# Who issues the reads of turned attention weights, who loads and mixes a filter's branches, and in what order TensorE takes its work

## The chip, the cores and the metric

The kernel runs on one core of one Trainium2 chip. The time is device microseconds of one execution. Each core has TensorE (PE; its weight loads are listed as PEld), VectorE (DVE), ScalarE (ACT), GpSimd (POOL) and SyncE (SP), each with an instruction queue of its own that is worked off in order. A DMA is issued by an instruction in such a queue: here mostly SP's, some ScalarE's, a few GpSimd's. "Landing" is when all its bytes have arrived.

## What is computed

An image x of 2 x 128 x 64 x 64 goes through a group norm and a first layer (7 x 7 neighbourhood attention with layer norms and three small linear maps; it isn't touched by the change). The result, seen as 2 sequences of 4096 tokens with 128 features, goes through a second layer:

```python
t = _to_tokens(x)
t = t + _L1_attn_ref(_ln_t(t))        # whole attention, q = k = v, the diagonal masked
t = t + _L1_ffn_ref(_ln_t(t), ...)    # a spectral filter
```

The attention has no weights: `softmax(q q^T / sqrt(128)) q` over all 4096 tokens, the diagonal set to -1e9. As the scores are symmetric, the weights of block (a, c) of queries and keys, turned (transposed), are those of block (c, a).

The filter convolves the normed tokens with 16 filters (phi) and multiplies each result by a matrix of 128 x 128, once for the sequence and once for the sequence with alternating signs:

```python
out = jnp.einsum('btkd,k,kde->bte', U_plus, s, Mpp)
out = out + jnp.einsum('btkd,k,kde->bte', U_minus, s, Mpm)
```

There are four such branches (four sets of M_u, M_phi_plus, M_phi_minus), each on a shorter part of the sequence, and the outputs are summed with weights from a softmax over four numbers. The kernel mixes the branches' matrices with these weights before the filter is applied.

## The kernel before, in words

The kernel is one program, written with a scheduler: each engine's instructions are put in order by it, by the order in which they were written (an earlier one has the higher priority) and by when it believes their inputs to be there. Two things overrule it. `tc.keep_in_program_order(...)` puts one instruction behind the instruction written just before it on the same engine. `tc.manual_schedule(engines={...})` keeps the written order on the engines named, for all that is written inside it; the first layer (L861) and the convolution at the end (L1658) are written so.

The stages in the trace: the first layer of both images up to about 350 us; the attention of image 0 up to about 780; that of image 1 up to about 1280; a short tail; from about 1330 the filter's convolution, in written order on TensorE, up to the end.

**The attention** (`attention(b, fill)`, L902) goes over the 36 pairs (a, c), a <= c, of eight chunks of 512 tokens, row by row, each pair in four steps j. In a step:

- `coming_of` (L1010) calls `weights` (L917) for the *next* pair: a score matmul into a PSUM bank (`bank`, five buffers; L927, or L936 for a diagonal pair) and an exponential on ScalarE into a quarter of the tile `e` (L932 or L943). In 27 of the 28 pairs off the diagonal (the "far" ones) the last of four quarters is followed by `sent` (L953): the whole megabyte of `e` is written to a DRAM tile `eb`, by a DMA on ScalarE's queue (L956).
- The current pair's product with its weights as they are: "other" (L1049), summed over four steps in one PSUM buffer, then added to `xa` by VectorE (L1066, or copied, L1068). A diagonal pair goes onto "own" instead, the row's sum (L983, in `onto`).
- `pass_on(2)` (L1017) does what is due of earlier pairs. With `at` the step at which a pair's weights were sent: at `at + MOVE` it calls `moved` (L959), four DMAs on SP's queue that read `eb` back into `et` (two buffers) in another layout (L963, pinned); at `at + TURN` `turned` (L968), two transposes of 32 x 32 blocks on VectorE (L972, pinned); from `at + DELAY` on, up to two products a step of the turned weights onto "own" (L983, pinned). The row's last product is followed by `complete` (L986), which adds "own" to `xa` on VectorE (L989).
- `fill()` (L1362) takes one step of other work from generators: first the urgent ones (`after(b, c)`, L1080, for each completed chunk: transposes L1088, statistics with a `pow` on GpSimd L174, apply L191, transposes back L202, ScalarE's copy L1113, the filter's forward transform L1142 and L1155, ScalarE's copies `uo` L1120, GpSimd's sums and differences `ub` L1123, and SP's stores into DRAM `us`, L1127 and L1132), then a list `steps`. A generator that yields None ends the filler's step; one that yields True lets the next in the list go too.

For image 0 the list `steps` holds `drain()` (the rest of the first layer; it makes the buffers `tt[1]`, `tok[1]`, `cm[1]` at its end, L1395 to L1398), `branch_weights()`, `filters()` (the filters' own transform: `pn` loads L1289, matmuls L1325, GpSimd's fb and fn, stores) and `tokens(1)`. For image 1 it holds what was left, and `for_ffn()` (L1438): once chunk 0 of image 1 is through, `filter_matrices` (L1268), then the load of `inv` and the first four sets of blocks `ct` (L1424).

**Mixing** (`mixed`, L1251): for each of four groups of four filters, for plus and minus, for each of four branches i: a DMA on SP's queue loads four matrices, 256 KB, into a tile `st` (two buffers, tag "st"; L1256); GpSimd multiplies it by the branch's weight (L1259 for i = 0, straight into the result; L1263) and adds it to the result (L1264). Two branches make one step of the filler. After plus and minus of a group GpSimd forms their difference and sum (L1276, L1277) and multiplies each filter's matrix by its sigma (L1280, L1281): one more step. That makes 20 steps.

Of the kernel before, what the change touches and what calls it, by code (L numbers as in the profile page):

```python
# [8 lines left out]
F32 = mybir.dt.float32  # L9
AF = mybir.ActivationFunctionType  # L10
ALU = mybir.AluOpType
# [3 lines left out]
P = 128  # L15
# [6 lines left out]
KF = 16  # L22
NBR = 4
MASKED = -1.0e30
MOVE, TURN, DELAY = 3, 7, 8

DIAG = -1.0e6
QSCALE = DH ** -0.5
# [74 lines left out]
def kernel(  # L103
# [16 lines left out]
    nc = tc.nc  # L120
# [756 lines left out]
    with ap_:  # L877
# [24 lines left out]
        def attention(b, fill):  # L902
# [56 lines left out]
            def moved(eb):  # L959

                et = ep.tile([P, 4, 512], F32, tag="et", name="et", bufs=2)
                for q in range(4):
                    tc.keep_in_program_order(nc.sync.dma_start(  # L963
                        out=et[32 * q : 32 * q + 32], in_=eb[:, q].rearrange("(h p) r -> p h r", h=4)
                    ))
                return et
# [12 lines left out]
                nc.vector.tensor_copy(et[:, m], pt)  # L979

            def onto(own, n, out_, e, first, last):
                tc.keep_in_program_order(
                    nc.tensor.matmul(out_, lhsT=tok[b][:, n, :], rhs=e, start=first, stop=last, skip_group_check=True)  # L983
                )

            def complete(a, own):  # L986
                xs = xa[b][:, chunk(a)]
                if a:
                    nc.vector.tensor_tensor(xs, own, xs, ALU.add)  # L989
                else:  # L990
                    nc.vector.tensor_copy(xs, own)
                fill(CHUNKS[a])
# [11 lines left out]
                if (c, t) == (7, 3):  # L1004
                    complete(a, own)

            coming_, late, turns, owns = [], [], [], {}
            step = 0

            def coming_of(a, c, k, left, halves):  # L1010
# [6 lines left out]
            def pass_on(n):  # L1017

                while coming_ and coming_[0][0] + MOVE <= step:
                    at, eb, a, c = coming_.pop(0)  # L1020
                    et = moved(eb)
                    turns.append((at + TURN, et))
                    late.extend((at + DELAY, a, c, et, t) for t in range(4))
                while turns and turns[0][0] <= step:
                    turned(turns.pop(0)[1])
                while n and late and late[0][0] <= step:
                    _, a, c, et, t = late.pop(0)
                    pair_onto(owns[a], a, c, et, t)
                    n -= 1

            es, halves = [], []
            for k in range(4):
                es.append(weights(0, 0, k, es, halves))
            for i, (a, c) in enumerate(pairs):
                following = pairs[i + 1] if i + 1 < len(pairs) else None
                coming, halves = [], []
                if a != c:
                    other = ps_o.tile([P, 512], F32, tag="other", name="other")
                else:
                    owns[a] = ps_o.tile([P, 512], F32, tag="own", name="own", bufs=2)  # L1040
                for j in range(4):
                    if following:
                        coming.append(coming_of(*following, j, coming, halves))
                    n = 4 * CHUNKS[a] + j
                    turn = lambda v, o: v.rearrange(o, q=4) if far(a, c) else v
                    if a == c:
                        onto(owns[a], n, owns[a], es[j], j == 0, a == 7 and j == 3)
                    else:
                        nc.tensor.matmul(  # L1049
                            turn(other, "p (q r) -> p q r"), lhsT=tok[b][:, n, :], rhs=es[j],  # L1050
                            start=(j == 0), stop=(j == 3),
                        )
                    if a != c and not far(a, c):
                        if j == 0:
                            here = ep.tile([P, 4, 512], F32, tag="et", name="et", bufs=2)
                        turned_here(here, es, j)
                        late.append((step + 1, a, c, here, j))
                    pass_on(2)
                    fill()
                    step += 1  # L1060
                if a != c:
                    xs, ov = xa[b][:, chunk(c)], other
                    if far(a, c):
                        xs, ov = xs.rearrange("p (t q j) -> p q t j", t=4, q=4), ov.rearrange("p (q t j) -> p q t j", q=4, t=4)
                    if a:
                        nc.vector.tensor_tensor(xs, ov, xs, ALU.add)  # L1066
                    else:
                        nc.vector.tensor_copy(xs, ov)  # L1068
                es = coming
            while late or coming_:  # L1070
                step += 1
                pass_on(2)
                fill()
            complete(7, owns[7])


        spare = [tok[0][:, 0:4, :]]
# [128 lines left out]
        def branch_weights():  # L1206
# [37 lines left out]
            nc.vector.tensor_tensor(wt, wt, ys, ALU.add)  # L1244

            yield
            for _ in mixed(mu, m_u, nc.vector, False):
                pass
            yield

        def mixed(dst, src, eng, steps):  # L1251
            dst2 = dst.rearrange("p k e -> p (k e)")
            for i in range(NBR):
                st = sp.tile([P, 4, P], F32, tag="st", name="st")
                n = src.shape[1]
                nc.sync.dma_start(out=st[:, 0:n], in_=src[i].rearrange("k d e -> d k e"))  # L1256
                st2 = st[:, 0:n].rearrange("p k e -> p (k e)")
                if i == 0:
                    eng.tensor_scalar(dst2, st2, wt[:, 0:1], None, ALU.mult)  # L1259
                elif eng is nc.vector:  # L1260
                    eng.scalar_tensor_tensor(dst2, st2, wt[:, i : i + 1], dst2, ALU.mult, ALU.add)
                else:
                    eng.tensor_scalar(st2, st2, wt[:, i : i + 1], None, ALU.mult)  # L1263
                    eng.tensor_tensor(dst2, dst2, st2, ALU.add)  # L1264
                if i % 2 and steps:
                    yield
# [218 lines left out]
    with ExitStack() as cv:  # L1485
# [210 lines left out]
        b = NB - 1  # L1696
# [117 lines left out]
```

## Time and profile before

| | |
|---|---|
| median of 3 runs | 2092.68 us (2091.77 to 2095.08) |
| the profiled execution, its own time | 2097.21 us |
| its span, first to last instruction | 2095.5 us |
| mean granted TensorE clock | 0.963 |
| busy: PE, PEld, DVE, ACT, POOL | 1931.1, 1357.0, 910.3, 723.4, 682.4 us |
| chain that ended last, PE's share; POOL; DMA | 63%; 9%; 7% |
| et read issues (L963), SP, count | 216, median 0.42 us each |
| eb write issues (L956), ScalarE, count | 54, median 0.33 us each |
| branch loads (L1256), SP, count | 32 of 256 KB, and 4 of 192 KB |
| turned transposes (L972), VectorE | 108, mean 1.22 us |
| the mixing's multiply (L1263) and add (L1264) on GpSimd | 1.56 and 1.26 us each |

How to read it: an engine's busy time is the union of its instructions; matmuls overlap each other by their fill, so a record of 0.6 us can follow the one before by 0.43. A 32-bit matmul is two records. Idle time before an instruction is put down to what released it last. The granted clock tells what share of TensorE's full speed the throttle let through. A name such as `et<-eb` is output from input.

### The profile page before, as it was taken

The page shows a single profiled execution, that of the slowest core. Times are in us where ns is not written, and L with a number is a line of the kernel's source. Part 1 is how long each engine was busy: PE and PEld are TensorE (multiplying, and loading weights), DVE is VectorE, ACT ScalarE, POOL GpSimd, SP SyncE. Part 2 cuts the span into 40 slices and gives each one's busy share as a digit, 9 for nine tenths or more (in the row PEclk, how much of TensorE's full clock was granted, in tenths as well). Part 3 has the DMA queues.
Part 4 walks back from the last instruction along what each step waited for, and adds up shares of the span by engine and source line. Part 5 has one row for each costly group of instructions (what it writes and reads, how often), then busy time and mean ns, then how long its engine had stood idle before and what let it go on. Part 6 is the DMA issues. An engine that isn't in the chain of part 4 may idle for free.

```text
span 2095.5 us, 51013 instructions
## 1 busy us (share of the span) xinstructions
PE 1931.1 (92%) x20504; PEld 1357.0 (65%) x20504; DVE 910.3 (43%) x2874; ACT 723.4 (35%) x1686; POOL 682.4 (33%) x1054
## 2 busy tenths in 40 slices
PE   6899998998899999995388998999999999999998
PEld 4677775444444444442133444699999899999987
DVE  5799986543433343422123335333333334333332
ACT  3789885313222234121022232222222222222222
POOL 4367976243011123028751111022222112222211
PEclk8999999999999999998689998999999999999999
DMA  4222222676466536466356641322222123222211
GB/s 150 62 61 61 62 60 65 199 184 187 137 191 180 164 86 214 122 184 171 101 155 167 185 134 52 87 67 66 68 66 64 46 58 100 66 70 67 66 45 42
DMA packets 278379, 225.98 MB, mean 108 GB/s; under 512 B 122607, under 2 KB 241535, under 8 KB 270720
## 3 DMA queue, kind: packets, MB, share of 16 engines
q1 hardware_dynamic: 269442, 162.59, 31.2%
q10 hardware_dynamic: 8126, 58.04, 7.0%
q8 instruction: 163, 2.67, 0.5%
q0 software_dynamic: 576, 2.10, 0.3%
q14 instruction: 72, 0.59, 0.1%
HBM read 131.40 MB, written 91.25 MB: 106 GB/s over the span
## 4 chain that ended last, share of the span: by engine, by line
PE 63%; issue 11%; POOL 9%; DMA 7%; DVE 6%; SPq 2%; ACT 1%; POOLq 0%; DVEq 0%; ACTq 0%
PE acc L1542 27%; PE pc L1523 7%; PE own L983 6%; PE bank L927 5%; PE other L1049 5%; PE bank L349 2%; PE bank L559 2%; POOL ub L1123 2%; PE bank L202 1%; POOL st L1263 1%; DMA et<-eb 1%; DMA st<-in_m_plus_dram 1%; DMA us<-ub 1%; PE bank L1142 1%; DMA st<-in_m_minus_dram 1%
## 5 line engine op out<-in xcount | busy, mean ns | idle before, releaser
L1528 DVE COPY y<-pc 128x512 f32<-128x512 f32 x320 | 206.1, 686 | 349.2 <-PE pc L1523 349.0
L1542 PE MATMUL acc<-y,mpl 32*128 32x256 f32 x5120 | 324.3, 379 | 0.8 <-DVE af L1552 0.8
L1542 PE MATMUL acc<-y,mmi 32*128 32x256 f32 x5120 | 316.5, 375 | 0.0
L1528 ACT COPY y<-pc 128x512 f32<-128x512 f32 x320 | 171.9, 589 | 397.5 <-PE pc L1523 392.9
L1542 PEld LDWEIGHTS acc<-y,mpl 32*128 32x128 f32 x5120 | 289.4, 186 | 8.0 <-DVE af L1552 1.3
L1542 PEld LDWEIGHTS acc<-y,mmi 32*128 32x128 f32 x5120 | 290.9, 185 | 3.9
L983 PE MATMUL own<-et,tok 128*128 128x512 f32 x448 | 217.3, 622 | 62.6 <-DVE et L972 60.8
L932 ACT ACTIVATE e<-bank 128x512 f32<-128x512 f32 x216 | 128.8, 599 | 406.7 <-PE bank L927 394.8
L1553 POOL TENSOR_TENSOR af<-af 128x512 f32<-128x512 f32 x39 | 49.7, 1274 | 591.8 <-DVE af L1552 540.2
L927 PE MATMUL bank<-cm 128*128 128x512 f32 x432 | 225.2, 612 | 4.5 <-ACT uo L1120 4.5
L1049 PE MATMUL other<-e,tok 128*128 128x512 f32 x448 | 225.2, 599 | 4.2 <-DVE xa L1066 4.2
L1523 PE MATMUL pc<-ct,ut 32*128 32x256 f32 x2560 | 214.5, 380 | 3.9 <-DMA ut<-us 2.1
L983 PEld LDWEIGHTS own<-et,tok 128*128 128x128 f32 x448 | 86.2, 199 | 175.4 <-issue 94.3
L1523 PEld LDWEIGHTS pc<-ct,ut 32*128 32x128 f32 x2560 | 174.4, 188 | 10.4 <-DVE y L1528 3.9
L972 DVE STREAM_TRANSPOSE et<-et 128x1024 f32<-128x1024 f32 x108 | 127.7, 1219 | 105.1 <-DMA et<-eb 105.1
L174 POOL TENSOR_TENSOR ln_rs<-ln_rs,mhalf 128x4 f32<-128x4 f32 x24 | 24.4, 1017 | 404.9 <-DVE ln_rs L173 404.9
L1049 PEld LDWEIGHTS other<-e,tok 128*128 128x128 f32 x448 | 82.8, 192 | 103.1 <-issue 95.4
L1123 POOL TENSOR_TENSOR ub<-uo 128x256 f32<-128x256 f32 (+1 forms) x164 | 99.8, 641 | 100.5 <-ACT uo L1120 69.5
L927 PEld LDWEIGHTS bank<-cm 128*128 128x128 f32 x432 | 76.7, 195 | 76.8 <-issue 62.1
L546 ACT ACTIVATE p<-p,mn 128x196 f32<-128x196 f32 x256 | 114.4, 449 | 14.1 <-DVE mn L536 13.6
L1066 DVE TENSOR_TENSOR xa<-other,xa 128x512 f32<-128x512 f32 x42 | 28.9, 687 | 167.9 <-PE other L1049 167.7
L536 DVE CUSTOM_DVE_ANT_0 p<-bank,tab 128x196 f32<-128x196 f32 x256 | 76.4, 353 | 4.9 <-PE bank L523 4.7
(262 smaller groups left out, 2607.1 us busy)
## 6 DMA issues: line engine op xcount, KB each, us to landing
eb<-e ACTq DMA_DIRECT2D x54, 1024.0 KB
et<-eb SPq DMA_DIRECT2D x216, 256.0 KB
ut<-us SPq DMA_DIRECT2D x160, 128.0 KB
us<-ub SPq DMA_DIRECT2D x128, 128.0 KB
ct<-gs SPq DMA_DIRECT2D x320, 40.0 KB
vw<-vd SPq DMA_DIRECT2D x256, 49.0 KB
ct<-gs SPq DMA_DIRECT2D x320, 32.0 KB
vd<-v SPq DMA_DIRECT2D x128, 32.0 KB
```

The costliest lines, as they stand in the source:

```text
L536: nc.vector.tensor_tensor_reduce(t[name + "p"][:, h, :], t[name + "S"][h][:, 0:KEYS], tab[:, ci, h, :], 1.0, 3.0e38, ALU.add, ALU.min, t[n ...
L546: nc.scalar.activation(p, p, AF.Exp, bias=t[name + "mn"][:, h : h + 1], scale=-1.0, accum_out=t["den"][:, u, h : h + 1],)
L927: nc.tensor.matmul(ps.rearrange("p (q t j) -> p q t j", q=4, t=4), lhsT=cm[b][:, n * P : (n + 1) * P], rhs=keys.rearrange("p (t q j) -> p ...
L932: nc.scalar.activation(e, ps.rearrange("p (q r) -> p q r", q=4), AF.Exp, bias=0.0, scale=ASCALE)
L972: tc.keep_in_program_order(nc.vector.transpose(flat, flat))
L983: nc.tensor.matmul(out_, lhsT=tok[b][:, n, :], rhs=e, start=first, stop=last, skip_group_check=True)
L1049: nc.tensor.matmul(turn(other, "p (q r) -> p q r"), lhsT=tok[b][:, n, :], rhs=es[j], start=(j == 0), stop=(j == 3),)
L1123: adder[0].tensor_tensor(ub[:, sgn, 0:n], both[:, 0:n], both[:, n : 2 * n], op)
L1523: nc.tensor.matmul(pcs[j].rearrange("p (g o c) -> p o g c", g=4, o=2)[:, :, at], lhsT=ut[rows_, par, :], rhs=cv_[rows_], start=True, stop= ...
L1528: (nc.scalar.copy if j % 2 else nc.vector.tensor_copy)(y[:, :, :, 4 * kl + j, :], pcs[j].rearrange("p (g x k) -> p k g x", g=4, k=KF))
L1542: nc.tensor.matmul(acc[j][:, 0:256], lhsT=(mmi if l else mpl)[rows_, k, :], rhs=y[rows_, k, 2 * l : 2 * l + 2].rearrange("p s n x -> p (s ...
L1553: eng.tensor_tensor(af[:, 0:2], af[:, 0:2], af[:, 2:4], ALU.add)
```

## The change

Four edits. First, the reads of `et` are issued on ScalarE's queue instead of SP's, still pinned, and one step later (MOVE 4 instead of 3; TURN and DELAY stay). Second, TensorE's instructions of the attention are kept in written order: for image 1 from its first step, for image 0 from the step at which `tt[1]` exists; the products onto "own" are no longer pinned one by one. Third, `pass_on(2)` comes ahead of the step's own product in the first step of a pair, and behind it in the other three; and `fill()` is called four more times at the head of image 1's attention. Fourth, the 32 branch loads of the filter's matrices are issued on GpSimd's queue, one part ahead of the mixing, and each part (one branch) is a step of the filler of its own, with one more per group: 36 steps. The small `m_u` stays on SP and VectorE as before.

```diff
-MOVE, TURN, DELAY = 3, 7, 8
+MOVE, TURN, DELAY = 4, 7, 8
...
-                    tc.keep_in_program_order(nc.sync.dma_start(
+                    tc.keep_in_program_order(nc.scalar.dma_start(
                         out=et[32 * q : 32 * q + 32], in_=eb[:, q].rearrange("(h p) r -> p h r", h=4)
                     ))
...
             def onto(own, n, out_, e, first, last):
-                tc.keep_in_program_order(
-                    nc.tensor.matmul(out_, lhsT=tok[b][:, n, :], rhs=e, start=first, stop=last, skip_group_check=True)
-                )
+                nc.tensor.matmul(out_, lhsT=tok[b][:, n, :], rhs=e, start=first, stop=last, skip_group_check=True)
...
+            written = ExitStack()
             es, halves = [], []
             for k in range(4):
                 es.append(weights(0, 0, k, es, halves))
+                if b:
+                    fill()
...
                 for j in range(4):
+                    if tt[1] is not None and not ordered:
+                        ordered.append(written.enter_context(tc.manual_schedule(engines={mybir.EngineType.PE})))
                     if following:
                         coming.append(coming_of(*following, j, coming, halves))
...
+                    if j == 0:
+                        pass_on(2)
                     if a == c:
                         onto(owns[a], n, owns[a], es[j], j == 0, a == 7 and j == 3)
...
-                    pass_on(2)
+                    if j:
+                        pass_on(2)
                     fill()
                     step += 1
...
             complete(7, owns[7])
+            written.close()
...
+        def branch(src, i, eng):
+
+            st = sp.tile([P, 4, P], F32, tag="st", name="st")[:, 0 : src.shape[1]]
+            eng.dma_start(out=st, in_=src[i].rearrange("k d e -> d k e"))
+            return st.rearrange("p k e -> p (k e)")
 
         def filter_matrices(mpl, mmi):
 
-            for k0 in range(0, KF, 4):
-                for dst, src in ((mpl, m_plus), (mmi, m_minus)):
-                    yield from mixed(dst[:, k0 : k0 + 4, :], src[:, k0 : k0 + 4], nc.gpsimd, True)
-
+            parts_ = [(k0, dst, src, i) for k0 in range(0, KF, 4) for dst, src in ((mpl, m_plus), (mmi, m_minus)) for i in range(NBR)]
+            loaded = [branch(m_plus[:, 0:4], 0, nc.gpsimd)]
+            for at, (k0, dst, src, i) in enumerate(parts_):
+                if at + 1 < len(parts_):
+                    k1, _, src1, i1 = parts_[at + 1]
+                    loaded.append(branch(src1[:, k1 : k1 + 4], i1, nc.gpsimd))
+                st = loaded.pop(0)
+                dst2 = dst[:, k0 : k0 + 4].rearrange("p k e -> p (k e)")
+                nc.gpsimd.tensor_scalar(dst2 if i == 0 else st, st, wt[:, i : i + 1], None, ALU.mult)
+                if i:
+                    nc.gpsimd.tensor_tensor(dst2, dst2, st, ALU.add)
+                yield
+                if dst is mpl or i + 1 < NBR:
+                    continue
                 a, d = (m[:, k0 : k0 + 4, :].rearrange("p k e -> p (k e)") for m in (mpl, mmi))
```

More of the change, by code (lines that the diff above doesn't have):

```diff
@@ L1005, in pair_onto @@
                     complete(a, own)
-            coming_, late, turns, owns = [], [], [], {}
+            coming_, late, turns, ordered, owns = [], [], [], [], {}
             step = 0
@@ L1246, in branch_weights @@
             yield
-            for _ in mixed(mu, m_u, nc.vector, False):
-                pass
-            yield
[L1251 to L1266, printed above, removed]
@@ L1268, in filter_matrices @@
-        def filter_matrices(mpl, mmi):
-            for k0 in range(0, KF, 4):
-                for dst, src in ((mpl, m_plus), (mmi, m_minus)):
-                    yield from mixed(dst[:, k0 : k0 + 4, :], src[:, k0 : k0 + 4], nc.gpsimd, True)
+            mu2 = mu.rearrange("p k e -> p (k e)")
+            for i in range(NBR):
+                st = branch(m_u, i, nc.sync)
+                if i == 0:
+                    nc.vector.tensor_scalar(mu2, st, wt[:, 0:1], None, ALU.mult)
+                else:
+                    nc.vector.scalar_tensor_tensor(mu2, st, wt[:, i : i + 1], mu2, ALU.mult, ALU.add)
```

## The prediction

> **What bounds the kernel now.** First the page's slices (52.4 us each). TensorE is nearly full from the third slice on, with one pit, slices 19 and 20:
>
> ```profile
> PE   6899998998899999995388998999999999999998
> ...
> PEclk8999999999999999998689998999999999999999
> ```
>
> So the end is set by TensorE; a microsecond counts where TensorE stands still, or runs at a lower clock after standing. Next the busy time by stretches of the second attention (a full stretch first; the columns are the stretch, its length, PE, PEld, DVE, ACT and POOL busy with their instructions, PE's granted clock, DMA share, GB/s):
>
> ```profile
> 840.00:860.00 20.00, 20.00 (x48) 8.76 (x47) 6.82 (x19) 2.97 (x5) 0.00 (x0) 1.00 0.52 139
> 960.00:1080.00 120.00, 51.24 (x123) 21.48 (x122) 17.42 (x33) 12.21 (x22) 98.80 (x95) 0.70 0.49 135
> 1100.00:1140.00 40.00, 30.69 (x68) 12.74 (x67) 14.37 (x29) 4.89 (x9) 1.04 (x1) 0.91 0.59 146
> ```
>
> In 960 to 1080 GpSimd is busy 99 us of 120 and TensorE 51. The SP queue's timeline says why (start, length, queue, line):
>
> ```profile
> 988.59 1.86 SPq L963 DMA_DIRECT2D et<-eb  x4
> 994.09 7.83 SPq L1256 DMA_DIRECT2D st<-in_m_plus_dram  x2
> 1001.97 0.52 SPq L1424 DMA_DIRECT2D ct<-gs  x1
> 1003.07 4.95 SPq L1256 DMA_DIRECT2D st<-in_m_plus_dram  x2
> 1010.53 3.37 SPq L1256 DMA_DIRECT2D st<-in_m_minus_dram  x2
> 1014.01 1.87 SPq L963 DMA_DIRECT2D et<-eb  x4
> ```
>
> and TensorE's own:
>
> ```profile
> 968.79 3.70 PE L983 MATMUL own<-et,tok 128*128 128x512 f32 x8 [0.23 <-DVE et L972]
> 999.42 5.90 PE L983 MATMUL own<-et,tok 128*128 128x512 f32 x8 [26.92 <-DVE et L972]
> 1025.04 6.74 PE L983 MATMUL own<-et,tok 128*128 128x512 f32 x8 [19.72 <-DVE et L972]
> ```
>
> The reader is to see a lockstep. A turned weight tile (et) is read on SP's queue behind six branch loads (L1256). Each load waits for a slot that GpSimd frees only after its mixing. One read in 25 to 32 us is let through, and TensorE waits for each.
>
> To size it I take the matmul records: in full stretches 512 columns follow each other every 0.43 us (eight records in 3.43 us), fewer columns in proportion. What lies between starts beyond that is lost: 83.0 us in 960 to 1080 (slow clock included), 12.6 in 1100 to 1140, 11.5 in 540 to 580 and 22.3 in 420 to 500; all the rest of 500 to 1280 loses 44. Work from 1280 on (the tail and the convolution) isn't touched.
>
> **The change, part by part.** The sum is made against the profiled execution: 2097.2 us, span 2095.5. The median of the runs shown is 2092.7, so 4.5 us come off at the end.
>
> *Branch loads to GpSimd, one part a step.* SP loses 32 issues of 0.37 to 0.56 us, which cost nothing themselves; what goes is their wait, and the reads no longer stand behind it. So the 83.0 us go. What comes late next is GpSimd itself. Its mixing is 8 multiplies of 1.57 us, 24 pairs of 1.56 + 1.26, and 4 closings of 2 x 1.27 + 8 x 0.605: 12.6 + 67.7 + 29.5 = 110 us. New are 32 issues on GpSimd. The nearest row is L802, 0.59 us each, for 128 rows of 4 KB; a branch load is 512 pieces of 512 B, four times as many. Bounds: 0.59 and 4 x 0.59 = 2.35 us; I take 1.0, since the bytes are half. The queue behind a waiting GpSimd holds the `pow` of the layer norms (L174) and the sums ub (L1123); for these wait VectorE's z and then TensorE's transposes (L202), and ScalarE's copies uo. Before, this wait is 15.7 us once inside the pit. After: before chunk 1's statistics some 22 steps of mixing are queued, two groups of 27.5 us and about 8 more, with 20 issues 83 us; a load lands in 2.9 to 4.6 us here against 2.83 of mixing, so about 0.7 us more each, 97. TensorE needs z some 24 steps after the start of the mixing, a step being three 512-column matmuls of 2 x 0.43, 2.57 us: 62 us. That is 35 us late if nothing overtakes. But at most two parts are loaded at a time, so a small `pow` can be placed into a gap between loads; I take 15. For chunk 2 likewise 71 against 51, 20 at most; I take 10. Together **+25**, bounds 0 and 70 (35 + 20, and 15 for the dearest issue).
>
> *Reads issued by ScalarE.* 216 issues go from SP (0.42 us) to ScalarE (its own issue, L956, takes 0.33): 91 us over some 890, hidden, since ScalarE is busy 3 us of 20 in the full stretch above. Also gone is the read's place behind the us stores, which wait for GpSimd: in 1100 to 1140 that is most of 12.6 (**-10**), in 540 to 580 most of 11.5 (**-9**). In 420 to 500 the waits for the filters' lags and for GpSimd stay, since TensorE needs both; only reads behind L1289 are freed: **-4** of 22.3.
>
> New waits: on ScalarE the read waits for its eb write, and behind it stand the exponentials that TensorE waits for. A write's last packet is 3.5 to 9.9 us after its issue, and MOVE = 4 puts 4 x 2.57 = 10.3 us between: nothing, at most about 1 us at the slowest writes. The read itself is later: issued four steps after its write, with the turn three steps on. From a step's score matmul: 1.02 us, the exponential by 1.8, the next pair's write issued by 2.15, then the reads. A lone read's turn begins 7.6 us after the first issue (rows at 638.7 and 646.3). Now the next pair's 1 MB write (2.7 us of packets alone) is put on the same queue just ahead. Whether packets of one queue pass each other no row shows: bounds 0 and 2.7, I take 2.2. Turn at 12.0, two transposes of 1.2: 14.4. TensorE is there at 4 x 2.57 + 1.71 = 12.0: 2.4 late, every second pair, since a stall gives the next read its time. Of the 53 stretches between two writes 32 hold less TensorE work than 12.7 us: 32 x 1.2 = 38. Against that about half of the 44 smaller losses are waits of the same kind, and go with it: **+15**. Bounds: -20 (that half goes, nothing comes) and +45 (my sum over the stretches, 67, less 22).
>
> By the Trainium skill ("DMA: Bandwidth & Descriptors", "Issuing engines are not separate DMA queues") a second issuing engine saves only issue time; that would make this part worth nothing. The SP rows above speak against that: the wait sits in the queue, ahead of the DMA engines.
>
> By the Trainium skill ("SBUF — State Buffer", "Who interferes with whom") GpSimd cannot write descriptors while VectorE runs a 2-port operation, and its example, 0.62 us grown to 3.1, would put 80 us on GpSimd for 32 loads, some 50 more on the end. L802's issues took 0.54 to 0.81 beside VectorE's tensor_scalars, so I leave it out of the sum.
>
> *Written order on TensorE.* No instruction more. The products with turned weights are pinned already, so what loses freedom are scores, "other" and the filler. A transpose whose input is late now holds the scores behind it, and through them ScalarE. For it: two products are put ahead of "other" at j = 0, covering the 1.04 us waits for VectorE's xa add (L1066), of which the records have four. No row shows the order alone; bounds -10 (the 0.95 and 1.04 us waits) and +25 (one 0.7 us wait in each of 36 pairs); I take **+5**. Four filler steps before the second attention's first pair, and 36 mixing steps for 20, issue no new work and end well before the attention does.
>
> Sum: -83 + 25 - 10 - 9 - 4 + 15 + 5 = **-61**: 2036 for the profiled kind, **2032** as a median.
>
> **Rivals.** *All of the gain*: no GpSimd lateness, reads in time: -83 - 12 - 11 - 10 - 0 = -116, 1977. For it: GpSimd has 22 to 28 steps per row to work in. Against: 142 us of GpSimd work over some 45 steps of 2.57, 116.
>
> *GpSimd becomes the bound*: issues at 2.35 us make 185 us of mixing; +70 in place of 25: 2077. For it: the 15.7 us wait for `pow` in the pit. Against: it is the whole of the bounds at once.
>
> *Reads too late, slower than before*: one mechanism, the read behind the write on ScalarE's queue, and TensorE unable to go round it. Two reads that overlapped at 660.9 needed 9.2 us to the last packet where one alone needs 6.7. With that much more on top, a pair is 2.4 + 2.5 = 4.9 late, 2.5 on the mean, over 54 pairs 132, less 22: +110 for +15, 2127. Even lies where reads cost 76 us over the smaller losses now, (76 + 22) / 54 = 1.8 us per pair.
>
> *The change doesn't do what it says*: the loads still hold something that TensorE needs at once, GpSimd's queue in SP's place, and the pit only changes its name: about 2090.
>
> **Numbers.** Forecast (2005 to 2060) 0.50; all of the gain 0.15; GpSimd bound (2060 to 2088) 0.19; no difference 0.05; slower 0.11. A measurement of this kernel can tell about 0.2% (4 us) from no change. Faster 0.84, same 0.05, slower 0.11. The range, 1985 to 2088, leaves out the best end of the second case and the slower one.
>
> **What would show it.** Right: in the second attention no stretch of 20 us with TensorE under 12; reads issued within 13 us of their write; loads on GpSimd of about 1 us; waits of TensorE for L202's z of 5 to 15 us while mixing runs; short waits for et, 1 to 3 us, every second pair. Wrong: waits for et of over 3 us at every pair (then the slower rival), GpSimd busy 95% with issues over 2 us, or ScalarE standing at a read while scores wait.

## The result: slower, and the profile after

The changed kernel takes **2213.32 us** (median of 4 runs, 2210.27 to 2223.75) against 2093.87 for the kernel before on the same chip: ratio 1.058, 95% interval 1.0544 to 1.0617. The prediction was 2032, faster; the sign is wrong, and the time lies beyond its range. The profiled execution took 2212.86 us, its span 2210.9, 115.4 more than before; its mean granted clock is 0.946. (Lines of the changed kernel from L955 on are numbered a little differently: own L982, other L1054, `uo` L1127, stores `us` L1134, branch loads L1266, products L1279, sums L1281.)

The slices that answer to those shown of before, 55.3 us each:

```profile
PE   7999998789898998885608989899999999999998
...
PEclk8999999999999999997858999899999999999999
```

The pit is still there. It has moved to slices 19 to 21, and one slice in it is empty; besides, the slices ahead of it hold 7s and 8s where before had 9s. By stretches (columns as before: stretch, length, PE, PEld, DVE, ACT, POOL, clock, DMA share, GB/s):

```profile
840.00:860.00 20.00, 14.82 (x57) 6.66 (x56) 5.82 (x23) 5.58 (x12) 7.37 (x12) 0.99 0.65 197
1100.00:1160.00 60.00, 0.00 (x0) 0.00 (x0) 0.00 (x0) 0.00 (x0) 53.42 (x52) 0.50 0.16 48
500.00:640.00 140.00, 126.04 (x391) 59.13 (x391) 55.77 (x157) 38.28 (x70) 23.61 (x40) 0.96 0.60 161
```

For 60 us no engine but GpSimd works. In 500 to 640, where no branch is mixed, TensorE is busy 126.0 of 140 us; before it was 132.6. So there are two losses. First TensorE's waits, before and then after (line waited at, releaser: us, times, longest):

```profile
PE own L983 <- DVE et L972: 60.8, 12, 26.9
PE bank L202 <- DVE z L191: 30.6, 6, 15.7
```

```profile
PE own L982 <- DVE et L972: 103.8, 27, 16.1
PE bank L202 <- DVE z L191: 85.1, 4, 71.6
```

The waits for turned weights were to go; there are now 27 where there were 12. The wait for z holds one of 71.6 us. The timelines of TensorE, GpSimd and VectorE show it (L173 on VectorE writes what the `pow` reads):

```profile
1089.66 1.02 PE L1054 MATMUL other<-e,tok 128*128 128x512 f32 x2
1162.30 1.16 PE L202 MATMUL bank<-ident,z 128*128 128x128 f32 x4 [71.62 <-DVE z L191]
```

```profile
992.19 1.57 POOL L1279 TENSOR_SCALAR mpl<-st,wt 128x512 f32<-128x512 f32 x1
994.05 0.85 POOL L1266 DMA_DIRECT2D st<-in_m_plus_dram  x1 [0.29 <-POOL mpl L1279]
...
1087.70 0.16 DVE L173 TENSOR_SCALAR ln_rs<-ln_mv 128x4 f32<-128x4 f32 x1
...
1098.08 1.56 POOL L1279 TENSOR_SCALAR st<-st,wt 128x512 f32<-128x512 f32 x1 [2.73 <-DMA st<-in_m_plus_dram]
...
1160.15 0.60 POOL L1292 TENSOR_SCALAR mmi<-mdiff,sg 128x128 f32<-128x128 f32 x1
1160.72 1.04 POOL L174 TENSOR_TENSOR ln_rs<-ln_rs,mhalf 128x4 f32<-128x4 f32 x1
```

GpSimd mixes from 992.19 to 1160.75, with only 4.4 us of the sums `ub` in between, and the `pow` (L174) of chunk 1's layer norm comes behind the very last of it, 168.5 us after the start. Its input is there only at 1087.9, so the `pow` itself waits 72.9 us. It doesn't slip into a gap: at 1098.08 GpSimd has been idle for 2.73 us, for a load, with the input of the `pow` there for 10 us. Before, the `pow` came 130.0 us after the mixing's start (921.6), in the middle of it, and waited 14.4 us:

```profile
1036.65 0.58 DVE L173 TENSOR_SCALAR ln_rs<-ln_mv 128x4 f32<-128x4 f32 x1
1051.63 1.04 POOL L174 TENSOR_TENSOR ln_rs<-ln_rs,mhalf 128x4 f32<-128x4 f32 x1
1053.10 1.64 POOL L1263 TENSOR_SCALAR st<-st,wt 128x512 f32<-128x512 f32 x1 [0.43 <-DMA st<-in_m_minus_dram]
```

Landmarks divide the 115.4 us: the second attention's first write is 46.6 us later (837.2, before 790.6), so that much is lost where nothing is mixed; up to the mixing's start another 24.0; from there to chunk 1's `pow` 38.5; all the rest 6.3.

ScalarE's timeline shows the other loss (ACTq are its DMA issues; the bracket holds the idle time ahead of an instruction and what ended it):

```profile
610.86 0.34 ACTq L956 DMA_DIRECT2D eb<-e  x1
611.38 3.78 ACTq L963 DMA_DIRECT2D et<-eb  x4
615.20 0.60 ACT L932 ACTIVATE e<-bank 128x512 f32<-128x512 f32 x1 [4.37 <-DMA us<-ub]
...
980.94 14.28 ACTq L963 DMA_DIRECT2D et<-eb  x4
995.32 1.07 ACT L1127 COPY uo<-bank 128x512 f32<-128x512 f32 x2 [14.94 <-DMA ct<-gs]
```

The write of the next pair and the read of this one stand back to back. The read's four issues take 3.78 and 14.28 us, and what stands behind them on ScalarE waits, put down to transfers (`us`, `ct`) that it does not use.

### The profile page after: what moved, and what is told of

Read it like the earlier page. It is cut to its first block, busy times and chain, and to the rows that moved or that the text cites. A ratio compares the mean times of both kernels' runs of the same rounds, so it can differ in the third digit from the quotient of the medians.

```text
span 2210.9 us, 50930 instructions
## 1 busy us (share of the span) xinstructions
PE 1949.0 (88%) x20504; PEld 1359.1 (61%) x20504; DVE 910.6 (41%) x2874; ACT 721.0 (33%) x1686; POOL 708.4 (32%) x1086
## 4 chain that ended last, share of the span: by engine, by line
PE 60%; DMA 11%; POOL 10%; DVE 7%; issue 6%; ACTq 2%; ACT 2%; SPq 1%; DVEq 0%; POOLq 0%
PE acc L1553 25%; PE own L982 8%; PE pc L1534 6%; DMA et<-eb 6%; PE bank L927 4%; PE other L1054 3%; DVE et L972 2%; PE bank L349 2%; POOL ub L1130 2%; DMA st<-in_m_plus_dram 2%; ACTq L963 2%; POOL st L1279 1%; PE bank L559 1%; DMA us<-ub 1%; PE bank L202 1%
## 5 line engine op out<-in xcount | busy, mean ns | idle before, releaser
L982 PE MATMUL own<-et,tok 128*128 128x512 f32 x448 | 241.1, 663 | 104.1 <-DVE et L972 103.8
L927 PE MATMUL bank<-cm 128*128 128x512 f32 x432 | 230.3, 615 | 12.5 <-ACT uo L1127 11.3
L1054 PE MATMUL other<-e,tok 128*128 128x512 f32 x448 | 232.2, 602 | 5.5 <-DVE xa L1074 5.4
L982 PEld LDWEIGHTS own<-et,tok 128*128 128x128 f32 x448 | 89.3, 208 | 231.4 <-DVE et L972 115.2
L174 POOL TENSOR_TENSOR ln_rs<-ln_rs,mhalf 128x4 f32<-128x4 f32 x24 | 24.4, 1017 | 429.0 <-DVE ln_rs L173 428.9
L1054 PEld LDWEIGHTS other<-e,tok 128*128 128x128 f32 x448 | 81.8, 193 | 100.5 <-issue 84.1
L202 PE MATMUL bank<-ident,z 128*128 128x128 f32 x252 | 43.9, 298 | 86.3 <-DVE z L191 85.1
L546 ACT ACTIVATE p<-p,mn 128x196 f32<-128x196 f32 x256 | 114.4, 449 | 14.4 <-DVE mn L536 13.8
L202 PEld LDWEIGHTS bank<-ident,z 128*128 128x128 f32 x252 | 31.5, 148 | 113.8 <-issue 95.6
```

The costliest lines, as they stand in the source:

```text
L202: nc.tensor.transpose(ps[:, j * P : (j + 1) * P], src[:, j, :], ident)
L546: nc.scalar.activation(p, p, AF.Exp, bias=t[name + "mn"][:, h : h + 1], scale=-1.0, accum_out=t["den"][:, u, h : h + 1],)
L927: nc.tensor.matmul(ps.rearrange("p (q t j) -> p q t j", q=4, t=4), lhsT=cm[b][:, n * P : (n + 1) * P], rhs=keys.rearrange("p (t q j) -> p ...
L1054: nc.tensor.matmul(turn(other, "p (q r) -> p q r"), lhsT=tok[b][:, n, :], rhs=es[j], start=(j == 0), stop=(j == 3),)
```

## The experiments

Each was timed beside the kernel before, whose medians there were 2091.2 to 2094.8; brackets hold the 95% interval of the ratio. Differences between runs are of medians, so some 3 us of them can be that spread. In the expectations, G is the theory that GpSimd's mixing costs the time, R that the reads do; Q, S and W are three causes for the reads, told there.

### One part at a time

**The reads alone** (kernel before, with):

```diff
-MOVE, TURN, DELAY = 3, 7, 8
+MOVE, TURN, DELAY = 4, 7, 8
-                    tc.keep_in_program_order(nc.sync.dma_start(
+                    tc.keep_in_program_order(nc.scalar.dma_start(
```

> The kernel before with the first edit alone: reads of et issued by ScalarE, MOVE 4. Theory G (the second attention is bound by GpSimd's mixing, and TensorE loses most where its written order makes it wait for a layer norm's pow behind the mixing): the reads add a few us at each pair but no longer stand behind branch loads; the pit of 83 us only changes its releaser, 2080 to 2125. Rival R (the reads behind the next pair's write on ScalarE's queue cost by far the most): 2160 to 2200.

Measured 2191.31, ratio 1.0481 [1.0464, 1.0499]: R's band holds. This edit alone costs 100 us; the whole change costs 119.

**The mixing alone** (kernel before with the new `filter_matrices`):

> The kernel before with the last edit alone: branch loads on GpSimd, one part a step. Theory G: mixing takes some 165 us of GpSimd in place of 150, the reads on SP go free, TensorE waits for pow at L202 but the scheduler puts other work ahead of it: 2070 to 2110. Rival R: the mixing is no loss and the pit is gone: 2010 to 2040.

Measured 2109.88, 1.0092 [1.0076, 1.0108]. Its waits of TensorE:

```profile
PE bank L202 <- DVE z L191: 110.0, 6, 92.9
...
PE own L983 <- DVE et L972: 10.4, 9, 4.2
```

The reader sees a swap: 50 us of waits for turned weights are gone (60.8 to 10.4), as predicted, and 79 us of waits for z have come (30.6 to 110.0). The input of the `pow` is there 70.2 us after the mixing's start, and the `pow` comes after 163.6.

**The written order, with the third edit** (`manual_schedule` on TensorE, `pass_on` ahead of "other", the four calls of `fill()`; reads on SP, old mixing):

> The written order of TensorE in the attention alone, reads on SP at MOVE 3 and the old mixing. Taking it out of the changed kernel changed nothing (2216 against 2213 us): if it costs nothing here either, 2085 to 2100 us. Rival: the order that the scheduler finds is worth something while the reads come in time, 2105 to 2125 us.

Measured 2129.7, 1.0171 [1.0151, 1.0191]: dearer than both bands, nearer to the rival's. No run has the written order without the third edit, so the 36 us are of both. Waits for turned weights grow from 60.8 to 90.1 us:

```profile
PE own L982 <- DVE et L972: 90.1, 15, 20.0
```

**The change without its new mixing:**

> The changed kernel with the old mixing: branch loads on SP, two parts a step. Theory G: the pow comes some 130 us after the mixing's start instead of 168, so TensorE's long wait at L202 shrinks from 72 to about 35 us: 2165 to 2185. Rival R: the reads cost the same as in the changed kernel: 2195 to 2215.

Measured 2197.56, 1.0506 [1.0488, 1.0525]: R's band holds. The pit is now one of turned weights again (TensorE waits 148.7 us for them and 12.9 for z), so the new mixing moves the wait and costs 16 us net. Against the reads alone (2191.3) the second and third edit together cost 6 us here.

**The change without the written order** (the third edit stays):

> The changed kernel without TensorE's written order (the products with turned weights pinned as before). Theory G: the 72 us wait at L202 is partly filled with scores and products, 2130 to 2165. Rival R: the products are pinned either way and wait for et, 2190 to 2215.

Measured 2215.61, 1.0598 [1.0579, 1.0617]: no difference from the changed kernel.

**The change without the reads' edit** (reads on SP, MOVE 3):

> The changed kernel without its first edit: the reads on SP at MOVE 3, with GpSimd's loads and mixing and the written order as changed. Alone, the written order cost 36 us and the mixing 16. If the two add up: 2135 to 2155 us, and the reads are worth 60 to 80 of the changed kernel's 120. If the written order cost what it cost because of SP's queue, which the loads leave with the new mixing: 2100 to 2125 us.

Measured 2149.9, 1.027 [1.0247, 1.0293]. Order and mixing add up (36 + 18 against 55), so the reads' edit makes 63 of the change's 119 us. It costs 100 alone: the three overlap, and the second and third edit, 36 us alone, cost 6 once the reads come late (2197.6 against 2191.3).

### What makes the reads dear

**MOVE 4 alone, the reads on SP:**

> The kernel before with MOVE at 4: the read is placed one step later, and SP still issues it. Theory S (the later step is what costs): at or over 2150 us, a fall of TensorE by 2 to 4 us ahead of own<-et in every second pair. Theory Q (the read queued behind the next pair's write in ScalarE's queue) and theory W (ScalarE held, in order, at reads that wait): 2085 to 2105 us, since here a read is neither behind a write on one queue nor on ScalarE.

Measured 2082.87, 0.9952 [0.9937, 0.9967].

**ScalarE alone, MOVE 3:**

> The kernel before with the reads on ScalarE's queue, placed at their old step (MOVE 3). Theory Q: the read comes just behind the following pair's write all the more, 2120 to 2160 us. Theory W: ScalarE reaches the read earlier and is held there longer, at or over 2190 us, with exponentials and copies of ScalarE that wait for the write's landing. Theory S: 2095 to 2120 us, since the placing is that of before.

Measured 2109.15, 1.0068 [1.005, 1.0086]. So neither half costs what both do: -10 and +16, against +100. S's band holds here, but S falls by the run before, where it asked for 2150; the bands of W and Q are both missed. The expectation was also wrong on the place: at MOVE 3 one read of 54 stands within 3 us behind a write, with the reads alone at MOVE 4 38 of 54 do.

**One more step for the turn and the product:**

```diff
-MOVE, TURN, DELAY = 3, 7, 8
+MOVE, TURN, DELAY = 4, 8, 9
```

> The kernel before with the reads on ScalarE's queue, MOVE 4, and the turning and the own matmuls one step later each (8 and 9 where 7 and 8 stood), so that the turned tile has about 5 us more. Theory Q: the 2 to 3 us of lateness that the shared queue costs are covered, 2110 to 2150 us. Theory W: the stalls of ScalarE at reads that wait stay, 2165 to 2195 us. Theory S: 2100 to 2140 us.

Measured 2154.02, 1.0288 [1.0271, 1.0304]: 37 of the 100 us come back, less than Q wanted.

**The read ahead of the next pair's write** (the reads alone, but the loop that issues them is called at the head of the step):

```diff
+                    reads()
                     if following:
                         coming.append(coming_of(*following, j, coming, halves))
```

> The kernel with the reads alone moved (ScalarE's queue, MOVE 4), except that in its step the read is written ahead of the next pair's write instead of behind it; step, queue and engine stay. Theory Q (a read that stands behind a write of 1 MB in one queue comes late): 2095 to 2135 us, no read within 3 us behind a write, the shortfall ahead of own<-et back at that of before. Theory W (ScalarE held at reads that wait for something): at or over 2165 us, as with the read behind the write, since ScalarE still stands at each read.

Measured 2098.95, 1.0026 [1.0014, 1.0038]: 92 us back for the read's place within one step on ScalarE. Q's band holds and W's falls. But the read now comes ahead of that step's exponential too, and the next run parts the two.

**The same, but between the fourth exponential and the write:**

```diff
+                    reads()
                     coming_.append((step, sent(halves[0]), a, c))
```

> The kernel with the reads alone moved (ScalarE, MOVE 4, at 2191 us), with one swap on ScalarE: the read stands just ahead of the next pair's write, where it stood just behind it. Both come after the fourth exponential of that pair, so the read stays some 5 us later than in the run where it comes ahead of that exponential (2099 us). If standing behind the write (its packets in the way, and four issues of 2.5 us in place of 1.3) is most of the 92 us between those two: 2100 to 2130 us, with the last packet at 6.8 us instead of 8.8. If the place behind the exponentials is most of it: 2150 to 2180 us, with the last packet at 6.8 us all the same.

Measured 2140.12, 1.0213 [1.0193, 1.0232], between the two bands. ScalarE in this run:

```profile
652.68 0.60 ACT L932 ACTIVATE e<-bank 128x512 f32<-128x512 f32 x1 [7.71 <-PE bank L927]
653.54 0.60 ACT L932 ACTIVATE e<-bank 128x512 f32<-128x512 f32 x1 [0.26 <-PE bank L927]
653.62 1.77 ACTq L963 DMA_DIRECT2D et<-eb  x4
655.48 0.39 ACTq L956 DMA_DIRECT2D eb<-e  x1
```

The read, though its data lie in DRAM, is issued only after two exponentials, the first of which stood 7.71 us for a score matmul. On SP it doesn't stand behind them.

**The write on SP, the read behind the exponentials on ScalarE:**

```diff
-                nc.scalar.dma_start(out=eb.rearrange("p q r -> p (q r)"), in_=eh)
+                nc.sync.dma_start(out=eb.rearrange("p q r -> p (q r)"), in_=eh)
```

> The kernel with the reads alone moved (ScalarE, MOVE 4, at 2191 us), except that SP issues the writes: the read stands at the same place on ScalarE, but no write is ahead of it in its queue. If the shared queue is what costs: TensorE's shortfall ahead of own<-et falls from 99 us to 30 or less, the read's last packet is 6.6 to 7 us after its first issue instead of 8.8, and the time is 2095 to 2135 us (up to 20 more than with the read ahead of the write, since the writes now stand behind loads on SP). If it is the place on ScalarE, four issues and a wait behind the write's step, whatever the queue: 2165 to 2200 us.

Measured 2169.8, 1.0356 [1.033, 1.0382]. The band of "the place, whatever the queue" holds, but swap shows that the place is not all. Medians over the first attention's 27 pairs, from the records, in us ("four issues" is from the first issue's start to the fourth's):

| | write to read | four issues | first issue to last packet | median time |
|---|---|---|---|---|
| before (SP, MOVE 3) | 9.1 | 1.3 | 6.7 | 2093 |
| SP, MOVE 4 | 13.2 | 1.4 | 7.0 | 2083 |
| ScalarE, MOVE 3 | 7.9 | 1.3 | 6.8 | 2109 |
| ahead of the exponential | 8.6 | 1.3 | 6.8 | 2099 |
| ahead of the write | 11.4 | 1.3 | 6.8 | 2140 |
| write on SP | 12.4 | 1.3 | 8.9 | 2170 |
| behind the write (reads alone) | 14.0 | 2.5 | 8.8 | 2191 |
| changed kernel | 13.6 | 2.5 | 8.7 | 2213 |

From 2099 to 2140 the read only comes later, behind the exponential: 41 us. From 2140 to 2191 it comes behind the write: 51 us. The 1 MB write issued in the same moment (0.5 us ahead of the read or behind it, at the median) makes the read 2.1 us longer whichever queue it is on (8.9 and 8.8 against 6.8); in the run with the write on SP the 8 reads with no write within 3 us took 6.9 at the median. The shared queue adds 1.2 us to the four issues; the time is 21 us longer, part of which can be the writes' own place on SP. TensorE's waits for turned weights up to 840 us follow: 6.2 us before, 7.5 with the read ahead of the exponential, 11.1 ahead of the write, 24.5 behind it. On SP a read that lands as late costs nothing. There ScalarE does not stand at it: from a pair's write to its first own product 29.9 us pass at the median (MOVE 4 on SP), 21.7 with the read ahead of the exponential. This loss of ScalarE's lead is a reading of the records, not an experiment of its own.

**MOVE 3 in the changed kernel:**

> The changed kernel with MOVE back at 3: everything else of the change is in. It tests theory Q in the changed kernel itself. Q: the reads no longer come behind a write, 2120 to 2150 us, about the 80 us that the same edit gave without the rest of the change (2191 to 2109); TensorE's wait of 72 us for the power behind the mixing stays. If the cost in the changed kernel is another than the read behind the write, it stays over 2180 us.

Measured 2130.68, 1.0176 [1.0151, 1.02]: 83 us back, as Q says; the wait for z stays (88.8 us at the longest). It is also 19 below the change with the reads on SP (2149.9), so ScalarE as the issuer is worth something there; MOVE 4 turned that into +63.

### What makes the mixing dear

**Products and sums on VectorE, loads and the rest as before:**

```diff
-                    yield from mixed(dst[:, k0 : k0 + 4, :], src[:, k0 : k0 + 4], nc.gpsimd, True)
+                    yield from mixed(dst[:, k0 : k0 + 4, :], src[:, k0 : k0 + 4], nc.vector, True)
```

> The kernel before with the products and sums of the second image's branch matrices on VectorE, the closing sums and differences still on GpSimd and the loads still on SP. It moves 96 of GpSimd's instructions off the engine whose work lies from 920 to 1071 us. If the pace of GpSimd's mixing is what made SP wait in the pit of the second attention (960 to 1080 us): 2020 to 2055 us, the pit gone and chunk 1's power no longer waiting. Rival: SP's waits there are for the loads' landing and the read of the turned weights, whoever mixes: 2080 to 2100 us. Second rival: VectorE is late with the maxima and z, over 2110 us.

Measured **2062.34**, 0.9849 [0.9833, 0.9866]: faster than both kernels. Of the pit:

```profile
960.00:1080.00 120.00, 69.64 (x178) 30.53 (x177) 41.04 (x70) 16.10 (x30) 31.17 (x45) 0.76 0.57 155
```

TensorE has 69.6 us of work in 960 to 1080 where it had 51.2, and GpSimd 31 where it had 99. The `pow` of chunk 1 waits 1.9 us. The band was just missed: the pit is smaller, not gone; one wait of 31.9 us ahead of a turned product, put down to a branch load, is left. (VectorE multiplies and adds in one instruction here, so 56 of GpSimd's instructions become 32 of VectorE's, not 96.)

**The mixing alone, with VectorE for products and sums; GpSimd still issues the loads:**

> The kernel with only GpSimd's loads of branch matrices, except that the products and sums are on VectorE; the loads are still issued by GpSimd. Theory G (chunk 1's power stands behind GpSimd's mixing): the wait of 93 us for z goes, as does SP's pit, 2030 to 2060 us. Rival: GpSimd still is held at each load until its buffer comes free, and the power still stands behind the loads: 2090 to 2115 us.

Measured 2075.7, 0.9916 [0.989, 0.9941], 34 below the same with GpSimd's arithmetic. The wait for z falls from 110.0 to 21.1 us, and the `pow`, which waited 93.4 us for GpSimd in the mixing alone, waits 3.4: it had stood behind the arithmetic. The gain expected was larger. The input of the `pow` comes 60 us later (1050.9 against 991.3), and the next waits took some:

```profile
PE other L1049 <- DVE xa L1066: 29.6, 6, 10.7
PE own L983 <- DVE et L972: 27.1, 10, 15.2
PE bank L202 <- DVE z L191: 21.1, 6, 7.5
```

VectorE is now late with `xa` and the turns. It also has 56 instructions of mixing here, product and sum apart, against 32 in the run before (35 us against 22), so the 13 us between 2075.7 and 2062.3 can't be put down to the loads' issuer alone.

**VectorE's mixing with MOVE 4 on SP:**

> The kernel with the products and sums on VectorE (2062 us) and the read one step later on SP (2083 us alone, 10 less than before). If the two gains lie in different stretches: 2048 to 2058 us. If both come out of the same pit: 2058 to 2066 us.

Measured 2073.12, 0.9898 [0.9876, 0.9921]: above both bands. The two gains don't add; it is even 11 above VectorE's mixing alone, and why stays open.

**VectorE's mixing with the reads ahead of the exponential:**

> The reads on ScalarE's queue ahead of the next pair's write (2099 us) together with the products and sums on VectorE (2062 us with the reads on SP). If SP's pit was the reads and the loads in one queue, both together free it: 2045 to 2060 us, below either. If ScalarE's stand at its reads stays the price of some 5 to 15 us that they had alone: 2065 to 2080 us.

Measured 2079.62, 0.9924 [0.9899, 0.9948], in the second band: together they are 17 us slower than VectorE's mixing with the reads on SP.

### Why another queue did not free the reads

In the run with the reads ahead of the exponential (2099 us) TensorE waited little for turned weights, but 55.7 us for exponentials, in the old pit. ScalarE there:

```profile
1006.48 9.20 ACTq L963 DMA_DIRECT2D et<-eb  x3
1015.73 0.60 ACT L932 ACTIVATE e<-bank 128x512 f32<-128x512 f32 x1 [30.23 <-DMA st<-in_m_minus_dram]
...
1032.03 14.99 ACTq L963 DMA_DIRECT2D et<-eb  x4
1047.06 2.55 ACT L932 ACTIVATE e<-bank 128x512 f32<-128x512 f32 x5 [24.82 <-DMA st<-in_m_plus_dram]
```

The read is on ScalarE's queue, the branch loads (`st`) on SP's, and still one waits for the other. The instruction records tell how; each transfer reports its landing on a semaphore, and waits first for one:

```
1003.53 SP  st<-in_m_plus_dram   semaphore=107
1006.48 ACT et<-eb  waits $S[107]  semaphore=107
1012.43 SP  st<-in_m_minus_dram  semaphore=103
1015.37 ACT et<-eb  waits $S[103]  semaphore=103
1038.18 SP  st<-in_m_plus_dram   semaphore=105
1040.96 ACT et<-eb  waits $S[105]  semaphore=105
```

The three loads landed at 1006.46, 1015.35 and 1040.94, and each of the three reads was issued 0.02 us later. Eight semaphores (100 and 102 to 108) go round among SP's and ScalarE's transfers; GpSimd's have others. A read's issue waits until the last user of its semaphore has landed, here a branch load that waited for GpSimd. The two rows of the changed kernel are not both of this kind: of the 14.28 us at 980.94 most is two such waits (for a `us` store and a `ct` load, landed at 986.80 and 994.88), but at 611.38 the semaphores of the two longest issues (1.67 and 1.18 us) were free when these began, and the time is that of issues behind the write.

To test it, the loads were taken off these queues:

**The reads ahead of the exponential, loads issued by GpSimd, arithmetic on VectorE:**

> The reads on ScalarE ahead of the next pair's write (2099 us alone), the branch matrices loaded by GpSimd and mixed by VectorE (2076 us alone), so that SP has neither the reads nor the loads. With the reads alone on ScalarE, TensorE still waited 56 us for exponentials, held behind reads whose issue waited for a branch load. If that is because their transfers share completion semaphores on SP's and ScalarE's queues, it goes with the loads: at most 25 us of waits for exponentials, 2045 to 2065 us. Rival: the reads are held by something else, or VectorE is the next bound: 2070 to 2085 us.

Measured 2088.0, 0.9982 [0.9967, 0.9997]: above both bands. But its reads in the pit are no longer held:

```profile
981.87 1.76 ACTq L963 DMA_DIRECT2D et<-eb  x4
...
1034.45 1.76 ACTq L963 DMA_DIRECT2D et<-eb  x4
```

From 965 to 1080 us no read's four issues take more than 2.3 us. In the run with VectorE's mixing and the loads still on SP (2080 us) one there took 24.82 us, and its last issue waited for a branch load. So the loads did hold the reads. What that was worth is another matter. TensorE's waits for exponentials in the three runs (the first; with VectorE's mixing; with the loads on GpSimd too):

```profile
PE other L1054 <- ACT e L932: 55.7, 4, 18.6
```

```profile
PE other L1054 <- ACT e L932: 5.9, 1, 5.9
```

```profile
PE other L1054 <- ACT e L932: 6.6, 1, 6.6
```

They were gone before the loads left SP, with VectorE's mixing; so this run doesn't show that the holds alone cost the 55.7 us. Nor is the coupling gone, since at 940 us a read is still held 16.76 us, by `us` stores and `ct` loads on SP. TensorE now waits for VectorE (27.8 us for turned weights, 14.9 for `xa`, 14.5 for quarters of `e` that VectorE copies), and the run with both parts put elsewhere is hardly better than before.

## Why the prediction was wrong, point by point

Two steps failed: the `pow` that was to slip into a gap of the mixing, and the size of the reads behind the next pair's write. Part by part, forecast and measured alone: the mixing -58 and +18, the reads -8 (+15 with the -10, -9 and -4) and +100, the order with the third edit +5 and +36. Together they make 119, not 154.

1. **The pit, -83 and +25.** That SP's lockstep would go was right (60.8 us of waits for turned weights became 10.4 with the mixing alone). The step that failed is "a small `pow` can be placed into a gap between loads; I take 15". No gap was used, though there were some (2.73 us of idle GpSimd at 1098, the input there): all 32 parts of the mixing and their closings stood ahead of the `pow`, not "some 22 steps". With the mixing alone, where the step can be read cleanly, the input came 70.2 us after the start (62 was taken) and the `pow` after 163.6, not 97. In the changed kernel it was 95.7 and 168.5, as the reads held TensorE too; TensorE waited 71.6 us. "One part a step" is an order of priority; the order on GpSimd that came of it put the whole mixing first, paced by its loads. With the mixing alone z costs 79 us more than before; the upper bound was 70. The issue, by contrast, was well sized: 0.75 to 0.90 us against 1.0.
2. **The reads, +15, bounds -20 and +45.** The mechanism was named, as the slower rival: the read behind the next pair's write. Its size failed: +100 alone, +63 within the change. The mis-sized term is 32 stretches at 1.2 us; the runs make it 100 us over 54 pairs, 1.9 us each. The transfer term was nearly right (8.8 us against 6.7, so 2.1, where 2.2 was taken). The place behind the next pair's last exponential was in the sum, but only as 1.8 us after a score matmul that comes on time; the runs price it at 41 us. The exponentials there wait for TensorE's scores (7.71 us in the row shown). The read comes 14.0 us after its write at the median, where four steps of 2.57, 10.3 us, were taken.
3. **"Nothing, at most about 1 us" for ScalarE's wait at a read.** Wrong. The write was indeed long landed, but a read's issue also waits for a completion semaphore that an unrelated transfer holds, up to 14.28 us for four issues in the changed kernel. This is also why ScalarE's queue did not part the reads from the loads. The prediction's own sign, "ScalarE standing at a read while scores wait", had it right.
4. **-10, -9 and -4 for other stretches.** They can't be seen in the changed kernel: in 500 to 640 TensorE has 126.0 us of work where it had 132.6, and 1100 to 1140 fell into the 71.6 us wait.
5. **The written order, +5, bounds -10 and +25.** With the third edit, which the term counted too, +36; with the new mixing still about that (55 for both); with the reads at MOVE 4 six. Which of the two edits costs it no run tells. My reading, untested: an order fixed in advance lets nothing past a product whose turned tile is late, which matters where a few tiles are late, and less where nearly all are.
6. **The rules cited.** That a second issuing engine only saves issue time (the Trainium skill, "DMA: Bandwidth & Descriptors", "Issuing engines are not separate DMA queues") was argued away in the prediction. At the old step, ScalarE as issuer made +16 alone and -19 within the change: the rule's "nothing" lies between the two, and what made +63 out of it was the place in the queue, of which the rule says nothing. The trap of the Trainium skill ("SBUF — State Buffer", "Who interferes with whom"), descriptors held up by VectorE, did not show in the issues: 32 loads took 0.75 to 0.90 us each, even with VectorE doing the mixing. (The example of the prediction, 0.62 us grown to 3.1, stands on the same page under "A bandwidth-pool intuition that's wrong (but worth ruling out)" and is of a whole transfer.)
7. **The chances.** The slower rival had 0.11, at 2127. It assumed that SP's pit would still be won; with the `pow` behind the mixing that gain was gone too, and the two losses came together.

## What to carry to other kernels

Before moving a DMA to an idle engine's queue, list what stands ahead of it there: here a read behind the last exponential of the next pair inherited that exponential's wait for TensorE, and a megabyte written in the same moment lengthened it by a third (6.8 to 8.9 us). Before putting work on a helper engine, look for the one small instruction on it that the bounding engine needs, and ask what would let it past: here 1 us of `pow`, its input ready, stood 73 us behind what was left of the mixing. Splitting a change into its parts is not enough where they interact; -10 and +16 made +100.

## What the runs showed of the hardware

- A 1 MB write issued in the same moment lengthens a 1 MB read, on one queue or two: the read's last packet at 8.8 and 8.9 us instead of 6.8.
- On one queue the four issues behind a write take 2.5 us from the first to the fourth, instead of 1.3.
- Transfers on SP's and ScalarE's queues are coupled by the completion semaphores that the program shares among them: the issues of one read took 14.99 us from first to last, and 24.82 us with VectorE's mixing; in the same stretch at most 2.3 us once the loads were on GpSimd.
- GpSimd issues a load of 256 KB (512 pieces of 512 B) in 0.75 to 0.90 us.
